# Group-norm coefficients of an input in fewer stages, averaged straight to the partition groups, with the third group's chain 24 steps later: a four-direction scan kernel on one core

## The chip, the cores and the metric

The kernel runs on one core of a Trainium2 chip. The metric is the device time of one execution in microseconds, median of the runs; lower is better. Engines are called PE (TensorE), DVE (VectorE), ACT (ScalarE), POOL (GpSimd) and SP (SyncE, which here only issues DMAs).

## The reference, cut to what matters

The input `x` is 32 x 48 x 64 x 128 (batch, channel, height, width), float32. Two layers do the same thing with different weights: the layer's input is group-normalised (16 groups of 3 channels), four recurrent scans run over it (down and up over the 64 rows with one set of weights, right and left over the 128 columns with two more), and the result is added to the layer's input.

```python
def _gn(v, G=16, eps=1e-5):
    g = v.reshape(B_, G, C_ // G, H_, W_)
    m = jnp.mean(g, axis=(2, 3, 4), keepdims=True)
    s = jnp.var(g, axis=(2, 3, 4), keepdims=True)
    return ((g - m) / jnp.sqrt(s + eps)).reshape(v.shape)

def step(w, b):
    def f(carry, inp):
        nxt = inp + _conv1d(carry, w, b)      # 5 taps over the other axis, 48 channels to 48
        return (nxt, nxt)
    return f
...
x = x + _L0_conv_ref(_gn(x), ...)             # down, up, right, left
x = x + _L1_conv_ref(_gn(x), ...)
```

A step needs the whole step before it, so the scans are serial: 63 + 63 row steps and 127 + 127 column steps for each layer and batch group.

## The kernel before, in words

**Tiling.** The batch of 32 is cut into four groups of 8 images (`GB = 8`, called the first to the fourth group below, `g` = 0 to 3 in the code). Row scans take one group at a time, column scans a pair of groups. The order of these phases is the list `PHASES` (L75): rows of group 0, rows of group 1, columns of the pair (0, 1), rows of group 2, and so on through both layers, 2286 steps in all. A vector of one step (8 of 48 channels by width or height folded in) lies as three tiles of 128 partitions by 128 elements (`NG = 3`); `step` (L654) makes the next vector with nine matrix products (two matmul records each in the profile) into three PSUM tiles, and three DVE additions (L674, PSUM plus bias plus the input vector) that write it back into the arena in SBUF. The next step's products read that.

**The order of the work.** Everything beside the scan is written into an agenda by hand: `at(t, fn, ...)` (L744) says that `fn` is issued just before scan step number `t`, counted through all phases (`starts` holds each phase's first number: 0, 126, 252, 506, ...). `spread(t, gen, every)` (L747) issues a generator's pieces, one at each `yield`, `every` steps apart. `catch_up` (L1082) issues what is due before each step, and `in_order` (L204) makes every engine execute its instructions in exactly the order in which they are issued. An engine's instruction that has to wait therefore holds up all that is queued behind it on that engine, the scan's own products and additions included.

**Statistics of an input.** Group norm of layer 0 needs mean and variance of each channel group of `x`. `InputStats` (L330) gathers them per channel and image:

- For the first group DVE does it (`take`, L343: `bn_stats` on pieces of 512 elements), before the scans start; eight `bn_aggr` (L378) at the end make mean and variance of each image, in the tile `mv_x`.
- For the other groups ACT does it (`take_others`, L349: a sum, L365, and a sum of squared deviations, L357, of each piece), spread over earlier phases; DVE turns the sums into mean and variance in three pieces of work (L383 to L385, L388 to L391, L393 to L398).

**From statistics to coefficients.** `scaling` (L263) then averages over the partitions of a channel group and spreads the result to the layout in which the scans hold a vector. `average` (L270) is a matrix product with `mask_sb`, whose entry is one over the number of partitions in the group where two partitions belong to the same group; `expand` (L274) is three products with `maskp`, which is the same mask with its columns rearranged (`spread_masks`, L253) for the three tiles of a vector. The chain for an input of layer 0 (`n == 1`, one mask), each stage ending at a `yield`:

1. PE: average of the means (L282).
2. DVE: copy to SBUF, `mean_c` (L285).
3. PE: expand (L287).
4. DVE: copy to SBUF, `mean` (L290); deviation from the average, squared, plus the variance (L295, L296, L297).
5. PE: average of that (L299).
6. DVE: copy, `var_c` (L302).
7. PE: expand (L304).
8. DVE: add epsilon (L307); ACT: square root (L310).
9. An empty stage, then DVE: reciprocal and a refinement (L314 to L319), scale and offset (L326, L327).

`ps` is one PSUM tile that holds all of these products. For results of layer 0, which feed layer 1, the same function runs with three masks (`n > 1`).

**Who uses the coefficients.** `scale_at_once` (L547, on DVE for the first four rows) and `scale_rows` (L535, on ACT, L543) apply them to rows in the arena before these are scanned. In `first_group` (L945), all of the start is written out: loads of `x` by image (`take_batch`), a permuted copy by POOL (`permute`, L491, its copies L500), a store to `xin` in DRAM (`put_out`) and a load of rows from there (`move_rows`); the first eight rows come by a matrix product instead (`rows_by_product`, L997).

**Around the third group.** `plan_input` (L757) plans loads, permuted copies and statistics of the other groups. For the third group (`g` = 2) the eight pieces are due from step 252 + 16 on, 13.5 steps apart; the last line of `plan_input` (L775) starts its `scaling` at the last piece's time plus `work + lag` = 12 plus 8. These steps lie in the first column phase, whose left scan begins at step 379. In the same stretch `plan_cols` (L812) plans what is done with the left scan's results: from step 379 + 34 on, POOL adds the residual to each unit of 128 x 2048 elements (`add_residual`, L599, L602), a quarter of the width at a time from the right, six units a quarter, and ACT and DVE take the result's statistics from them. The third group's rows are first scaled at step 506 - 13.

Of the kernel before, what the change touches and what calls it, by code (L numbers as in the profile page):

```python
# [35 lines left out]
P = ODD + C  # L36
# [5 lines left out]
GB = 8  # L42
E8 = 8
FULL = 128
NG = E8 * C // FULL
# [46 lines left out]
def kernel(  # L92
# [8 lines left out]
    nc = tc.nc  # L101
# [158 lines left out]
    def stat_tile(shape, name, key):  # L260
        return stat_pool.tile(shape, F32, tag=name, name=f"{name}_{key}")

    def scaling(key, layer, g, averages, masks):  # L263


        n = len(masks)
        yield from averages(key)
        mean_p, var_p = averages.result

        def average(ps, rhs):  # L270
            for i in range(n):
                nc.tensor.matmul(ps, masks[i], rhs[:, i], start=i == 0, stop=i == n - 1)

        def expand(ps, rhs):  # L274
            for o in range(NG):
                nc.tensor.matmul(ps[:, o], maskp[:, o], rhs, start=True, stop=True)

        def small(name):
            return stat_tile([FULL, NG, GB], name, key)

        ps = ps_stat.tile([FULL, 2 * NG + 2, GB], F32, tag="ps_stat", name=f"ps_{key}")
        average(ps[0:P, 0], mean_p)  # L282
        yield
        mean_c = stat_tile([P, GB], "mean_c", key)
        nc.vector.tensor_copy(mean_c, ps[0:P, 0])  # L285
        yield
        expand(ps[:, 1 : 1 + NG], mean_c)  # L287
        yield
        mean = small("mean")
        nc.vector.tensor_copy(mean, ps[:, 1 : 1 + NG])  # L290
        at = mean if n > 1 else mean_c.unsqueeze(1)
        np_ = FULL if n > 1 else P
        spare = small("dev")
        dev = spare[0:np_, 0:n]
        nc.vector.tensor_tensor(dev, mean_p, at, ALU.subtract)  # L295
        nc.vector.tensor_tensor(dev, dev, dev, ALU.mult)  # L296
        nc.vector.tensor_tensor(dev, dev, var_p, ALU.add)  # L297
        yield
        average(ps[0:P, 1 + NG], dev)  # L299
        yield  # L300
        var_c = stat_tile([P, GB], "var_c", key)
        nc.vector.tensor_copy(var_c, ps[0:P, 1 + NG])  # L302
        yield
        expand(ps[:, 2 + NG :], var_c)  # L304
        yield
        var = small("var")
        nc.vector.tensor_scalar(var, ps[:, 2 + NG :], GN_EPS, None, ALU.add)  # L307

        std = small("std")
        nc.scalar.activation(std, var, AF.Sqrt)  # L310
        yield
        yield
        r0 = std
        nc.vector.reciprocal(r0, std)  # L314
        t0 = spare
        nc.vector.tensor_tensor(t0, var, r0, ALU.mult)
        nc.vector.tensor_tensor(t0, t0, r0, ALU.mult)
        yield
        nc.vector.tensor_scalar(t0, t0, -0.5, 1.5, ALU.mult, ALU.add)  # L319
        scale, offset = (  # L320
            stat_pool.tile(
                [FULL, NG, GB], F32, tag=f"{t}{layer}{g}", name=f"{t}{layer}{g}"
            )
            for t in ("scale", "offset")
        )
        nc.vector.tensor_tensor(scale, r0, t0, ALU.mult)  # L326
        nc.vector.scalar_tensor_tensor(offset, mean, -1.0, scale, ALU.mult, ALU.mult)  # L327
        coeffs[layer, g] = scale, offset

    class InputStats:  # L330
# [2 lines left out]

        def __init__(self, key, nv):
            self.nv = nv
            if nv:
                self.st = stat_tile([P, nv, NBN * 6], "bn", key)
            if nv < GB:
                self.sum, self.neg, self.dev2 = (
                    stat_tile([P, GB, NBN], f"{n}_x", key)[:, nv:] for n in ("sum", "neg", "dev2")  # L340
                )

        def take(self, i, nat, b):  # L343

            for n in range(nat.shape[-1] // BN):
                at = slice(6 * (i + n), 6 * (i + n + 1))
                nc.vector.bn_stats(self.st[:, b, at], nat[:, b, n * BN : (n + 1) * BN])

        def take_others(self, i, nat):  # L349
            k = nat.shape[-1] // BN  # L350
            for square in (False, True):
                for b in range(self.nv, GB):
                    for n in range(k):
                        at = b - self.nv, slice(i + n, i + n + 1)
                        piece = nat[:, b, n * BN : (n + 1) * BN]
                        if square:
                            nc.scalar.activation(  # L357
                                junk[0:P],
                                piece,
                                AF.Square,  # L360
                                bias=self.neg[:, at[0], at[1]],
                                accum_out=self.dev2[:, at[0], at[1]],
                            )
                        else:
                            nc.scalar.activation(  # L365
                                junk[0:P],
                                piece,
                                AF.Identity,
                                accum_out=self.sum[:, at[0], at[1]],
                            )  # L370
                if not square:
                    at = slice(i, i + k)
                    nc.scalar.mul(self.neg[:, :, at], self.sum[:, :, at], -1.0 / BN)

        def __call__(self, key):
            mv = stat_tile([P, 1, GB, 2], "mv_x", key)
            for b in range(self.nv):
                nc.vector.bn_aggr(mv[:, 0, b], self.st[:, b])  # L378
            yield
            if self.nv < GB:  # L380
                n = GB - self.nv
                mean = stat_tile([P, GB], "mean_x", key)[:, 0:n]
                nc.vector.tensor_reduce(mean, self.sum, mybir.AxisListType.X, ALU.add)  # L383
                nc.vector.tensor_scalar(mean, mean, 1.0 / (NBN * BN), None, ALU.mult)
                nc.vector.tensor_copy(mv[:, 0, self.nv :, 0], mean)  # L385
                yield
                dev = self.neg
                nc.vector.tensor_tensor(  # L388
                    dev, dev, mean.unsqueeze(2).to_broadcast([P, n, NBN]), ALU.add
                )  # L390
                nc.vector.tensor_tensor(dev, dev, dev, ALU.mult)  # L391
                yield
                nc.vector.scalar_tensor_tensor(  # L393
                    dev, self.dev2, 1.0 / BN, dev, ALU.mult, ALU.add
                )
                var = stat_tile([P, GB], "var_x", key)[:, 0:n]
                nc.vector.tensor_reduce(var, dev, mybir.AxisListType.X, ALU.add)
                nc.vector.tensor_scalar(mv[:, 0, self.nv :, 1], var, 1.0 / NBN, None, ALU.mult)  # L398
                yield
            self.result = mv[:, :, :, 0], mv[:, :, :, 1]  # L400
# [68 lines left out]
    x_masks = [mask_sb]  # L469
# [274 lines left out]
    def at(t, fn, *args):  # L744
        agenda.append((t, len(agenda), fn, args))

    def spread(t, gen, every):  # L747


        def go(t):  # L750
            if next(gen, "end") != "end":
                at(t + every, go, t + every)
                agenda.sort(key=lambda a: a[:2])

        at(t, go, t)

    def plan_input(g, times, work, lag, nats, perms):  # L757

        stats = InputStats(f"x{g}", 0)
        rows = nats[0].shape[-1] // W  # L760
        ahead, pieces_of = len(nats), rows * W // BN
        per = rows * W * GB // perms[0].shape[-1]
        for j, t in enumerate(times):
            nat = nats[j % ahead]
            if j == 0 and g > 1:
                at(t - 7, take_in, g, 0, nat)
            for i in range(per):
                perm, r = perms[i % len(perms)], i * rows // per
                at(t + i * work / per, permute, nat, r, perm, [nc.gpsimd])
                at(t + i * work / per + 4, put_out, g, 2 * rows * j + r, perm, rows)  # L770
            at(t + lag, stats.take_others, pieces_of * j, nat)
            if j + ahead < len(times):
                free = t + 7
                at(free, take_in, g, 2 * rows * (j + ahead), nat)
        spread(t + work + lag + (0, 2, 8, 5)[g], scaling(f"x{g}", 0, g, stats, x_masks), 1)  # L775

    def plan_rows(k, t0, prev):
        if k == 1:
# [166 lines left out]
    def first_group():  # L945
# [26 lines left out]
        for b in range(2 * GB):  # L972
# [3 lines left out]
            i, b = divmod(b, GB)  # L976
# [6 lines left out]
        stats = InputStats("x0", GB)  # L983
# [56 lines left out]
        spread_masks()  # L1040
        for b in range(GB):
            stats.take(NBN // 2, parts[1], b)
        for r in range(12, 16):
            put_row(0, r)
        move_rows(0, 8, 16, False)
# [100 lines left out]
```

## Time and profile before

| what | value |
|---|---|
| three runs | 4352.66, 4369.14, 4376.32 us; median 4369.14 |
| profiled execution | 4367.57 us, of which the span from first to last instruction is 4365.80 |
| granted PE clock, mean | 0.982 |
| PE busy | 4150.5 us (95%) |
| DVE, ACT, POOL busy | 2169.3, 1337.3, 888.3 us |
| DMA queues | 680.34 MB, most of it in packets under 512 B |
| first scan step starts | 102.13 us after the span's start |
| first column phase | right scan from 658.95, left scan from 917.88 to 1191 us |

The page of the profile gives each engine's busy time, then groups of instructions by source line. A timeline line reads: start in us from the span's start, duration in us, engine, line, operation, written tile <- read tiles, shapes, count, and in brackets the idle time of the engine just before and what ended it. A line with a count above one is several like instructions in a row, and its duration is from the first one's start to the last one's end. A list of waits gives the engine and line that waited, what it waited for, and the total in us, the number of times and the longest.

### The profile page before, as it was taken

The page shows a single profiled execution, that of the slowest core. Times are in us where ns is not written, and L with a number is a line of the kernel's source. Part 1 is how long each engine was busy: PE and PEld are TensorE (multiplying, and loading weights), DVE is VectorE, ACT ScalarE, POOL GpSimd, SP SyncE. Part 2 cuts the span into 40 slices and gives each one's busy share as a digit, 9 for nine tenths or more (in the row PEclk, how much of TensorE's full clock was granted, in tenths as well). Part 3 has the DMA queues.
Part 4 walks back from the last instruction along what each step waited for, and adds up shares of the span by engine and source line. Part 5 has one row for each costly group of instructions (what it writes and reads, how often), then busy time and mean ns, then how long its engine had stood idle before and what let it go on. Part 6 is the DMA issues. An engine that isn't in the chain of part 4 may idle for free. (4 is left out here: it accounts for less than half of the span.)

```text
span 4365.8 us, 90057 instructions
## 1 busy us (share of the span) xinstructions
PE 4150.5 (95%) x36632; PEld 4121.9 (94%) x36632; DVE 2169.3 (50%) x6558; ACT 1337.3 (31%) x2656; POOL 888.3 (20%) x859
## 2 busy tenths in 40 slices
PE   4899989989999999999999999999999999999992
PEld 2899989989999999999999999999999999999992
DVE  6444444446665444444446665444444444444443
ACT  1583201435785545100006764503000012110122
POOL 4561010324322020010004410000000024510352
PEclk9999999999999999999999999999999999999996
DMA  9999699866999989579307989839188049999999
GB/s 187 176 195 165 104 159 168 216 121 206 228 195 152 159 158 156 92 126 199 80 1 244 224 163 143 124 61 170 32 139 181 1 88 237 238 242 157 170 199 178
DMA packets 2112607, 680.34 MB, mean 156 GB/s; under 512 B 2000448, under 2 KB 2052032, under 8 KB 2072256
## 3 DMA queue, kind: packets, MB, share of 16 engines
q1 hardware_dynamic: 2014176, 582.29, 70.9%
q10 hardware_dynamic: 94816, 86.00, 9.7%
q0 software_dynamic: 3200, 6.30, 0.6%
q8 instruction: 288, 4.72, 0.5%
q14 instruction: 127, 1.04, 0.1%
HBM read 397.57 MB, written 295.99 MB: 159 GB/s over the span
## 5 line engine op out<-in xcount | busy, mean ns | idle before, releaser
L543 ACT ACTIVATE arena<-arena,offset,scale 128x256 f32<-128x256 f32 (+2 forms) x816 | 576.8, 800 | 391.1 <-DVE arena L674 145.7
L602 POOL TENSOR_TENSOR arena<-arena 128x2048 f32<-128x2048 f32 x80 | 362.9, 4550 | 1509.8 <-PE step_10l L665 484.9
L500 POOL COPY arena<-arena 112x256 f32<-112x256 f32 x458 | 270.5, 648 | 549.6 <-DMA arena<-in_x 277.2
L665 PE MATMUL step_00r<-arena,early 128*128 128x128 f32 x2286 | 259.0, 277 | 15.3 <-DMA arena<-upa 15.2
L665 PEld LDWEIGHTS step_00r<-arena,early 128*128 128x128 f32 x2286 | 258.3, 194 | 16.0 <-issue 15.3
L434 ACT ACTIVATE early<-arena 128x256 f32<-128x256 f32 x192 | 129.4, 674 | 468.7 <-DMA arena<-xin 328.6
L665 PE MATMUL step_01r<-arena,early 128*128 128x128 f32 x2286 | 258.5, 277 | 14.5 <-DMA arena<-upa 14.5
L665 PEld LDWEIGHTS step_01r<-arena,early 128*128 128x128 f32 x2286 | 258.1, 193 | 14.9 <-issue 14.6
L665 PE MATMUL step_00l<-arena,wleft 128*128 128x128 f32 x2286 | 258.6, 276 | 13.9 <-DVE arena L674 13.9
L665 PEld LDWEIGHTS step_00l<-arena,wleft 128*128 128x128 f32 x2286 | 257.7, 193 | 14.1 <-DVE arena L674 14.1
L665 PE MATMUL step_11r<-arena,early 128*128 128x128 f32 x2286 | 259.3, 277 | 7.8 <-DVE arena L674 7.8
L665 PEld LDWEIGHTS step_11r<-arena,early 128*128 128x128 f32 x2286 | 258.6, 194 | 8.4 <-DVE arena L674 8.2
L665 PE MATMUL step_10r<-arena,early 128*128 128x128 f32 x2286 | 256.0, 275 | 0.0
L665 PEld LDWEIGHTS step_10r<-arena,early 128*128 128x128 f32 x2286 | 255.7, 192 | 0.3
L665 PE MATMUL step_10l<-arena,wleft 128*128 128x128 f32 x2286 | 255.5, 275 | 0.0
L665 PE MATMUL step_11l<-arena,wleft 128*128 128x128 f32 x2286 | 255.5, 275 | 0.0
L665 PE MATMUL step_01l<-arena,wleft 128*128 128x128 f32 x2286 | 255.4, 275 | 0.0
L665 PEld LDWEIGHTS step_10l<-arena,wleft 128*128 128x128 f32 x2286 | 255.4, 192 | 0.0
L665 PEld LDWEIGHTS step_11l<-arena,wleft 128*128 128x128 f32 x2286 | 255.4, 192 | 0.0
L665 PEld LDWEIGHTS step_01l<-arena,wleft 128*128 128x128 f32 x2286 | 255.3, 192 | 0.0
L627 ACT COPY arena<-arena 128x256 f32<-128x256 f32 x172 | 99.5, 654 | 420.1 <-POOL arena L602 143.1
L365 ACT ACTIVATE early<-arena 112x512 f32<-112x512 f32 x192 | 121.1, 631 | 296.1 <-DMA arena<-in_x 226.8
(179 smaller groups left out, 7113.1 us busy)
## 6 DMA issues: line engine op xcount, KB each, us to landing
arena<-in_x SPq DMA_DIRECT2D x48, 768.0 KB, 12.7
xin<-arena SPq DMA_DIRECT2D x96, 384.0 KB, 5.6
arena<-xin SPq DMA_DIRECT2D x96, 384.0 KB, 8.2
mid<-arena SPq DMA_DIRECT2D x96, 384.0 KB, 7.7
arena<-mid SPq DMA_DIRECT2D x192, 192.0 KB, 4.4
upb<-arena SPq DMA_DIRECT2D x192, 192.0 KB, 3.9
arena<-upb SPq DMA_DIRECT2D x96, 384.0 KB, 11.7
arena<-xin SPq DMA_DIRECT2D x186, 192.0 KB, 4.3
```

Of the source, the lines that this page charges most:

```text
L365: nc.scalar.activation(junk[0:P], piece, AF.Identity, accum_out=self.sum[:, at[0], at[1]],)
L434: nc.scalar.activation(junk[:, 0:n], view[:, b], AF.Identity, accum_out=self.sum[:, i, j : j + 1])
L500: copy(dst[:, r, q], src[:, r0 + r, q])
L543: nc.scalar.activation(args[0], args[0], AF.Identity, bias=args[2], scale=args[1])
L602: eng.tensor_tensor(unit, unit, nat, ALU.add)
L627: copy(by_w(perm)[:, a], src[:, a])
L665: nc.tensor.matmul(part(whole(ps[o]), -s), weights[:, i, FULL * (o - NG * s - i + 1) : FULL * (o - NG * s - i + 2)], part(src(i), s), star ...
```

## The change

Three edits, all for inputs of layer 0 (`n == 1`); the results' path with three masks keeps its instructions and their order.

- In `scaling`, `expand` is applied to the means themselves, right after the average and in the same stage, and later to the deviations themselves; the average of the deviations and its copy `var_c` are gone. `mean` is copied from PSUM after the second expansion has been issued. The chain has three stages fewer.
- For the first group, the aggregate of each image (`bn_aggr`) is issued right after that image's last `bn_stats` (`aggregate`), and no longer for all eight at the end. `mv_x` becomes a tile of the object for all groups.
- In `plan_input`, the third group's `scaling` starts 32 steps after the last piece's `work + lag`, where it was 8.

```diff
         average(ps[0:P, 0], mean_p)
+        if n == 1:
+            expand(ps[:, 1 : 1 + NG], mean_p[:, 0])
         yield
         mean_c = stat_tile([P, GB], "mean_c", key)
         nc.vector.tensor_copy(mean_c, ps[0:P, 0])
         yield
-        expand(ps[:, 1 : 1 + NG], mean_c)
-        yield
+        if n > 1:
+            expand(ps[:, 1 : 1 + NG], mean_c)
+            yield
         mean = small("mean")
-        nc.vector.tensor_copy(mean, ps[:, 1 : 1 + NG])
+        if n > 1:
+            nc.vector.tensor_copy(mean, ps[:, 1 : 1 + NG])
...
-        average(ps[0:P, 1 + NG], dev)
-        yield
-        var_c = stat_tile([P, GB], "var_c", key)
-        nc.vector.tensor_copy(var_c, ps[0:P, 1 + NG])
-        yield
-        expand(ps[:, 2 + NG :], var_c)
+        if n == 1:
+            expand(ps[:, 2 + NG :], dev[:, 0])
+            nc.vector.tensor_copy(mean, ps[:, 1 : 1 + NG])
+        else:
+            average(ps[0:P, 1 + NG], dev)
+            yield
+            var_c = stat_tile([P, GB], "var_c", key)
+            nc.vector.tensor_copy(var_c, ps[0:P, 1 + NG])
+            yield
+            expand(ps[:, 2 + NG :], var_c)
         yield
...
+            self.mv = stat_tile([P, 1, GB, 2], "mv_x", key)
...
+        def aggregate(self, b):
+            nc.vector.bn_aggr(self.mv[:, 0, b], self.st[:, b])
...
         def __call__(self, key):
-            mv = stat_tile([P, 1, GB, 2], "mv_x", key)
-            for b in range(self.nv):
-                nc.vector.bn_aggr(mv[:, 0, b], self.st[:, b])
+            mv = self.mv
...
-        spread(t + work + lag + (0, 2, 8, 5)[g], scaling(f"x{g}", 0, g, stats, x_masks), 1)
+        spread(t + work + lag + (0, 2, 32, 5)[g], scaling(f"x{g}", 0, g, stats, x_masks), 1)
...
             stats.take(NBN // 2, parts[1], b)
+            stats.aggregate(b)
```

## The prediction

> **What bounds the kernel now.** I read the page first. TensorE (PE) is the bound by far: 36,632 matmul records, 4150.5 us of a 4365.8 us span.
>
> ```profile
> PE 4150.5 (95%) x36632; PEld 4121.9 (94%) x36632; DVE 2169.3 (50%) x6558; ACT 1337.3 (31%) x2656; POOL 888.3 (20%) x859
> ```
>
> The line doesn't say what a change is worth, only that PE's pauses are what can be won: 215 us, 61 of them ahead of the first scan step at 102.13. So I listed next what PE itself waits for (us in total, times, longest).
>
> ```profile
> PE step_00l L665 <- DVE arena L674: 13.9, 1, 13.9
> PE step_00d L665 <- DVE arena L674: 13.1, 2, 8.5
> PE ps_x L272 <- DVE mv_x_x L378: 12.1, 1, 12.1
> ...
> PE ps_x L272 <- DVE dev_x L297: 4.7, 1, 4.7
> ```
>
> The first is in the left scan of the first column phase, the others at the start. Why did VectorE (DVE) give nothing to step_00l? Its timeline there:
>
> ```profile
> 928.13 0.35 DVE L674 SCALAR_TENSOR_TENSOR arena<-step_00l,bd,arena 128x128 f32<-128x128 f32 x1 [0.30 <-PE step_00l L665]
> 940.14 0.22 DVE L383 TENSOR_REDUCE mean_x_x<-sum_x_x 112x8 f32<-112x64 f32 x1 [11.66 <-ACT early L365]
> 940.40 3.07 DVE L384 TENSOR_SCALAR mean_x_x<-mean_x_x 112x8 f32<-112x8 f32 x1
> 943.50 0.17 DVE L385 COPY mv_x_x<-mean_x_x 112x8 f32<-112x8 f32 x1
> ...
> 947.16 0.23 DVE L388 TENSOR_TENSOR neg_x_x<-neg_x_x,mean_x_x 112x64 f32<-112x64 f32 x1 [2.72 <-ACT early L357]
> ```
>
> The third group's reduce (L383) stands in DVE's queue after left step 4 (from 0; each step is 18 matmul records and 2.01 us) and waits for ScalarE's (ACT's) last sums; the scan's own adds (L674) stand behind it. And L384, eight elements wide, takes 3.07 us instead of 0.17. GpSimd (POOL) says why:
>
> ```profile
> 934.15 9.29 POOL L500 COPY arena<-arena 112x256 f32<-112x256 f32 x16 [16.70 <-DMA arena<-in_x]
> 1000.18 27.11 POOL L602 TENSOR_TENSOR arena<-arena 128x2048 f32<-128x2048 f32 x6 [56.74 <-PE step_00l L665]
> ```
>
> POOL's copies end at 943.44, L384 at 943.47. The second line matters for what follows: six residual additions without a gap, 4.52 us each, released by PE.
>
> **What the Trainium skill says.** "SBUF — State Buffer", section "Who interferes with whom": a DVE instruction with two SBUF inputs contends with a GpSimd instruction that reads SBUF, and a copy or tensor_scalar in a 2-port mode contends too; the first holds the shared pair for its whole instruction. "VectorE: DVE Perf Modes", section "Mode 2×_2P — use both read ports for one tensor", adds that PSUM sources can't use that mode. The trace agrees: L384 above; L295 (two SBUF inputs) 4.15 us at the start against 0.15 for the same line at 957.58; the PSUM copy L290 0.18 in the same POOL run; the scan's add (one input PSUM) 0.35 beside POOL. The trace adds what the page doesn't say, in two forms. In both cases just told DVE waited through the rest of POOL's run, many copies. In the second group's chain each of these waited for one copy only (0.64 us):
>
> ```profile
> 318.78 0.51 DVE L384 TENSOR_SCALAR mean_x_x<-mean_x_x 112x8 f32<-112x8 f32 x1
> ...
> 319.33 0.55 DVE L385 COPY mv_x_x<-mean_x_x 112x8 f32<-112x8 f32 x1
> ...
> 320.57 0.53 DVE L388 TENSOR_TENSOR neg_x_x<-neg_x_x,mean_x_x 112x64 f32<-112x64 f32 x1
> 321.13 0.56 DVE L391 TENSOR_TENSOR neg_x_x<-neg_x_x 112x64 f32<-112x64 f32 x1
> ```
>
> The two that starved (DVE passed over again and again) asked 0.06 and 0.10 us before POOL's next start (89.92, 940.50), these about 0.4 us or more before it (319.21, for one).
>
> **The change part by part.** I go by the profiled execution: 4367.57 us, span 4365.80; the median of the runs is 1.6 higher.
>
> *Start, first group.* (Times us from the span's start.) Seven of eight aggregates (L378: 1.97/8 = 0.25 us each) go into gaps of 1.5 to 5.8 us that bn_stats spends waiting for in_x: PE gets the averages 1.65 us sooner; uncovered they'd cost 1.7. One average with its copy (0.54 + 0.2 + about 0.1 of handing over) leaves the variance half, an expansion (1.42) leaves the way to L295. If L295 still starves until POOL ends at 93.98, only about 0.6 is left of this; if it waits copy by copy, the scan starts up to 4.6 sooner. (L297 at 88.4 after three copies, expansion to 89.9, L316 to L327 five copies' waits to 93.6, L554 3.5: 97.5 instead of 102.1.) Either way row 16 is late next; here are ACT's, DVE's and POOL's timelines, a fence each:
>
> ```profile
> 128.46 0.62 ACT L543 ACTIVATE arena<-arena,offset,scale 128x128 f32<-128x128 f32 x1 [7.90 <-DMA arena<-xin]
> 135.28 23.56 ACT L543 ACTIVATE arena<-arena,offset,scale 128x128 f32<-128x128 f32 x46 [2.26 <-DMA arena<-xin]
> ```
>
> ```profile
> 145.56 0.35 DVE L674 SCALAR_TENSOR_TENSOR arena<-step_00d,bd,arena 128x128 f32<-128x128 f32 x1 [9.76 <-ACT arena L543]
> ```
>
> ```profile
> 100.64 3.69 POOL L500 COPY early<-arena 112x256 f32<-112x256 f32 x4 [6.66 <-DMA xin<-early]
> ```
>
> ACT waits for rows that come through POOL's permutes and SP's queue, none of which needs the coefficients; PE's 8.54 us pause there swallows the gain. What passes: the four copies in the last line took 3.69 instead of 2.34 beside DVE's L554, and all later permutes follow without a gap. If L554 is done sooner, up to 1.35 comes back. I take -0.7, between -1.4 and 0.
>
> *Second and fourth group.* One PE average less, 0.13 each (step starts 324.34 to 324.47). The chain ends three steps sooner. For the second, L316 to L327 move from about 345 to about 339, into POOL's copies (332.0 to 341.5): one copy's wait each, as at 318.78, where a step grew by 0.10 to 0.14; about 0.3; starved, 3. The fourth has no POOL work near (1622.7 on). Together +0.1, between -0.3 and +3.
>
> *Third group, 24 steps later: what goes.* Step 5 starts at 927.93, step 8 at 950.24: 22.31 for three steps of 2.01 and an average of 0.13, so 16.15 was lost. ACT's statistics end at 947.1 and depend on in_x, not on PE. By the order of instructions of the changed kernel the reduce now stands after left step 28, natural start of 29 at 927.93 + 24 x 2.01 = 976: all is ready. With one average less: -16.3. The moved work issues no DMA; on ACT it passes no other instruction, on POOL and SP it has none; scale_rows needs the coefficients at step 493, the chain ends by 419.
>
> *What comes in its place.* Count from T, the end of left step 31 (about 982). POOL's L602 for quarter 3 waits only for that step's read of column 96: before, it began at 1000.18 when step 32 began at 1000.11. The residuals have landed by about 971, where the DMA engines fall idle, so it again starts at T + 0.07 and its operations end at about 4.6, 9.1, 13.6, 18.2, 22.7, 27.2. PE runs average and expansion (0.13 + 0.59) ahead of step 32; L295 to L297 follow DVE's adds of step 33, 0.55 into step 34: T + 0.72 + 4.02 + 0.55 = T + 5.3, inside the second operation, 3.7 before the next. The trace has no such DVE operation beside an L602. The lower bound is 0 (POOL might let go within its 4.5 us; no gain possible, as nothing is removed); the upper is the whole run. By the second group's rows I take one operation for each: L295 at 9.1, L296 at 13.6, L297 at 18.2. PE's next expansion, queued ahead of step 35, waits for L297, and DVE's adds of step 34 are queued behind it: step 35 starts at 18.2 + 0.05 + 0.6 = 18.85 instead of 7.34, a loss of 11.5. L316, near 25.7, waits once more to 27.2: 1.2. In all +12.7. Beyond 27.2 POOL waits for quarter 2. ACT's square root delays the result statistics behind it by some 12 us; POOL's next run is 60 us off, enough cover.
>
> Sum: -0.7 + 0.1 - 16.3 + 12.7 = -4.2: 4363.4, or 4365.0 by the median.
>
> **The rivals.** *The lock is no lock here* (0.17): POOL lets go within an operation. For it: no row shows L602 holding DVE. Against: seven rows with copies, and the page. -4.2 - 12.7 = -16.9: 4352.2.
> *Only L295 waits, the two behind it slip in* (0.13): L297 at 9.5, step 35 at 10.15, 2.8 lost, later 1.0: -13.1, 4356.0. Against it: 319.33 and 321.13, seconds in a row that waited again.
> *L295 starves through POOL's run* (0.2), on the other side: L297 at 27.65, step 35 at 28.35, 21.0 lost, nothing later: -0.7 + 0.1 - 16.3 + 21.0 = +4.1, 4373.2, slower. For it: the two starved rows. Against: they asked within 0.1 us of POOL's next start. It decides from a new wait of 16.9 us.
>
> **Numbers.** Forecast (one operation each) 0.5: 4365. A measurement of this kernel can tell about 0.5%, 22 us, from no change, and its three runs spread over 24 us. Range 4348 to 4379: from the lockless case to the starved one, and some 5 us of spread. Faster by over 0.5% needs the lockless case and luck, 0.11; slower 0.04; within, 0.85.
>
> **What would show it.** Right: no pause near 930; L295, L296 and L297 of the third group last some 3.8, 4.5 and 4.5 us, PE pauses near 989 to 1001 for dev; row 16 still waits for ACT near 145. Wrong: L295 at 0.2 us there (4352), or about 22 us (4373); the pause of row 16 gone, so that the start pays up to 4.6.

## The result, and the profile after

| | before | after |
|---|---|---|
| median of 20 runs each | 4366.91 us (4351.00 to 4383.66) | 4364.42 us (4353.77 to 4371.49) |
| ratio after to before | | 0.9993, 95% interval 0.9982 to 1.0004 |
| span of the profiled execution | 4365.8 us | 4362.4 us |
| first scan step starts | 102.13 us | 96.57 us |
| left scan of the first column phase starts | 917.88 us | 921.38 us |
| rows of the third group start | 1191.06 us | 1192.01 us |

There is no difference that the measurement can tell: its interval reaches some 0.11% to either side, where the forecast had allowed for 0.5%. The forecast was 4365.0. The time says little, then, on whether the sum behind it held, so I went through its parts. The page of the kernel after (busy time of the engines, first line):

```profile
PE 4148.9 (95%) x36624; PEld 4119.6 (94%) x36624; DVE 2178.5 (50%) x6554; ACT 1337.5 (31%) x2656; POOL 887.7 (20%) x859
```

PE has as much work as before: 2024 scan steps of 18 matmul records (eight row phases of 126 steps, four column phases of 254; the 2286 given as the number of steps further up is the number of records of one column scan), and the statistics' products. But DVE, with four instructions fewer, is busy 9.2 us longer: instructions that wait inside count as busy. What PE itself waits for (total, times, longest), in the list of waits of the kernel after:

```profile
PE step_00d L675 <- DVE arena L684: 17.1, 2, 11.2
...
PE step_01d L675 <- DVE arena L684: 13.1, 1, 13.1
PE ps_x L276 <- DVE dev_x L301: 12.7, 2, 11.0
```

Before's wait of 13.9 us in step_00l is no longer in the list. In its place PE waits 11.0 us for `dev_x` (L301 is before's L297, L299 and L300 its L295 and L296, L684 its L674). DVE's timeline of the kernel after shows both ends of the exchange:

```profile
980.14 0.21 DVE L393 TENSOR_REDUCE mean_x_x<-sum_x_x 112x8 f32<-112x64 f32 x1
980.39 0.17 DVE L394 TENSOR_SCALAR mean_x_x<-mean_x_x 112x8 f32<-112x8 f32 x1
...
991.07 3.71 DVE L299 TENSOR_TENSOR dev_x<-mv_x_x,mean_c_x 112x8 f32<-112x8 f32 x1
994.81 4.42 DVE L300 TENSOR_TENSOR dev_x<-dev_x 112x8 f32<-112x8 f32 x1
999.27 4.42 DVE L301 TENSOR_TENSOR dev_x<-dev_x,mv_x_x 112x8 f32<-112x8 f32 x1
1003.61 0.85 DVE L684 SCALAR_TENSOR_TENSOR arena<-step_00l,bd,arena 128x128 f32<-128x128 f32 x3
```

The reduce (L393, before's L383) has no idle time ahead of it now, where it had 11.66 us, and L394 takes 0.17 us where L384 took 3.07. But ten microseconds later three instructions, eight elements wide, take 12.5 us together. The scan's own additions (L684) come behind them. POOL's timeline of the kernel after:

```profile
936.77 9.47 POOL L510 COPY arena<-arena 112x256 f32<-112x256 f32 x16 [16.69 <-DMA arena<-in_x]
985.77 26.87 POOL L612 TENSOR_TENSOR arena<-arena 128x2048 f32<-128x2048 f32 x6 [39.53 <-PE step_00l L675]
```

The residual additions run from 985.77 without a gap, 26.87 / 6 = 4.48 us each, so that their ends lie near 990.2, 994.7, 999.2 and 1003.7. DVE's three instructions end at 994.78, 999.23 and 1003.69: each waited for the end of one POOL instruction.

What followed on PE is seen in its timeline, and in the table of windows, whose columns after the length are the busy times of the five engines, and PE's granted clock third from the end:

```profile
1003.74 1.45 PE L276 MATMUL ps_x<-dev_x,maskp 112*128 112x8 f32 x6 [10.96 <-DVE dev_x L301]
```

```profile
1005.70:1007.70 2.00, 2.00 (x11) 2.00 (x11) 0.17 (x1) 0.00 (x0) 2.00 (x1) 0.50 1.12 340
1007.70:1009.00 1.30, 1.30 (x8) 1.30 (x7) 0.53 (x2) 0.00 (x0) 1.30 (x2) 0.50 1.01 189
1009.00:1011.00 2.00, 2.00 (x20) 2.00 (x19) 1.05 (x4) 1.08 (x4) 2.00 (x1) 0.98 0.93 225
```

PE pauses for 10.96 us, and then works at half its clock from 1003.74 to about 1009, which loses another 2.65 us: 13.6 together. By the starts of the steps the loss is 13.8 (11.8 up to step 35, 2.0 in it).

At the start, the lines that answer those shown of before are, for DVE (the additions that wait for row 16) and POOL, a fence each:

```profile
142.00 0.35 DVE L684 SCALAR_TENSOR_TENSOR arena<-step_00d,bd,arena 128x128 f32<-128x128 f32 x1 [12.46 <-ACT arena L553]
```

```profile
99.56 2.40 POOL L510 COPY early<-arena 112x256 f32<-112x256 f32 x4 [6.77 <-DMA xin<-early]
```

SP issues the loads of row 16 and those after it; before and after:

```profile
121.65 19.88 SPq L200 DMA_DIRECT2D arena<-xin  x20
```

```profile
119.26 19.96 SPq L200 DMA_DIRECT2D arena<-xin  x20
```

The first step is 5.56 us sooner, but DVE waits longer for row 16 (12.46 us, where it was 9.76): of the 5.56, 3.56 are left there. POOL's four copies take 2.40 us instead of 3.69.

### The profile page after: what moved, and what is told of

Its sections match the earlier page's. It is cut to its first block, busy times and chain, and to the rows that moved or that the text cites. A ratio compares the mean times of both kernels' runs of the same rounds, so it can differ in the third digit from the quotient of the medians.

```text
span 4362.4 us, 90034 instructions
## 1 busy us (share of the span) xinstructions
PE 4148.9 (95%) x36624; PEld 4119.6 (94%) x36624; DVE 2178.5 (50%) x6554; ACT 1337.5 (31%) x2656; POOL 887.7 (20%) x859
## 6 DMA issues: line engine op xcount, KB each, us to landing
arena<-in_x SPq DMA_DIRECT2D x48, 768.0 KB, 12.8
```

## The experiments

My theory was the forecast's: the old loss in the third group is gone, and in its place three DVE instructions wait for one POOL addition each, because their inputs both lie in SBUF; that POOL run is all that keeps the change from gaining. The main rival: some other thing at the later place, or the shortened chain itself, holds the time up. In all ratios below, each kernel is compared with the kernel before on the same chip; before's medians there were 4358.88 us (first four), 4357.61 (next four) and 4359.90 (last three). The ratios and their intervals are those on record; they are not the quotients of the medians, from which they differ by up to 0.0006. Where nothing is said, a kernel computes all of the reference.

**The third group's chain elsewhere.** Three places beside the 32 of the change: ahead of POOL's run, four steps into a worse place, and between POOL's first run and its second.

```diff
-        spread(t + work + lag + (0, 2, 32, 5)[g], scaling(f"x{g}", 0, g, stats, x_masks), 1)
+        spread(t + work + lag + (0, 2, 20, 5)[g], scaling(f"x{g}", 0, g, stats, x_masks), 1)
```

(28 and 54 in the two others.)

> The changed kernel with the third group's chain 12 steps later than in the kernel before instead of 24 (offset 20). All of its DVE instructions then lie after ACT's last sums and before POOL's first residual addition. Port theory: no pause of PE between left steps 4 and 45, each of the chain's DVE operations at 0.15 to 0.3 us; the 13.9 us lost there by the changed kernel (11.8 ahead of step 35, 2.0 behind it) come back: 4364.4 - 13.9 = 4350.5 us. Rival (the pause comes with the shortened chain, since PE's second expansion now stands directly behind DVE's work, wherever the chain is put): the pause is there again, 4364 us.

Measured: 4346.20 us, ratio 0.9973 (0.9960 to 0.9986). All of the chain's operations took 0.15 to 0.29 us (947.38 to 969.6), POOL's additions began after them at 978.68, and PE had no pause in the left scan.

> The changed kernel with offset 28, four steps earlier than it has. The deviations (L299 to L301) then come ahead of POOL's first residual addition, the reciprocal's group (L324 to L335: five operations with two SBUF inputs or one in a 2-port mode) inside POOL's run. Port theory: L299 to L301 at 0.2 us; L324 and L325 wait for an addition each, and the three behind step 34's adds wait again: losses of about 8.1 + 2.0 + 7.6 + 2.0 = 19.7 us in place of 13.9, so worse than the changed kernel although nearer to where the statistics are ready: 4364.4 + 5.8 = 4370.2 us. Rival (shortened chain): 4364 us. Rival (any time after the sums are ready is free): 4350.5 us.

Measured: 4367.96 us, ratio 1.0020 (1.0011 to 1.0029), slower than before. The deviations were done ahead of POOL's run (from 979.84 on, 0.15 to 0.17 us each), and the second half of the chain was caught in it. POOL's and DVE's timelines of this kernel:

```profile
984.13 26.91 POOL L612 TENSOR_TENSOR arena<-arena 128x2048 f32<-128x2048 f32 x6 [43.03 <-PE step_00l L675]
```

```profile
988.88 4.28 DVE L324 TENSOR_TENSOR dev_x<-var_x,std_x 128x24 f32<-128x24 f32 x1
993.19 4.44 DVE L325 TENSOR_TENSOR dev_x<-dev_x,std_x 128x24 f32<-128x24 f32 x1
998.34 3.80 DVE L327 TENSOR_SCALAR dev_x<-dev_x 128x24 f32<-128x24 f32 x1
1002.17 4.44 DVE L334 TENSOR_TENSOR scale<-std_x,dev_x 128x24 f32<-128x24 f32 x1
1006.65 4.44 DVE L335 SCALAR_TENSOR_TENSOR offset<-mean_x,scale 128x24 f32<-128x24 f32 x1
```

Five instructions wait for five additions. Four steps earlier is 8 us worse, since five operations of the chain fall into the run where three did: the left scan took 278.7 us, 21.8 over its undisturbed 256.9, where the changed kernel's lost 13.8.

> The changed kernel with offset 54: the chain lies between POOL's first run of residual additions (six, ending about 27 us after left step 31) and its second (from left step 63 on). Port theory: no pause, 4350.5 us, the same as for offset 20, though it is the latest of all; ACT's square root stands behind the result statistics of three units and may come some us late without anybody waiting. Rival (the later the chain, the more it collides): 4364 us or more.

Measured: 4342.51 us, ratio 0.9967 (0.9955 to 0.9979). The chain ran from 1018.75 on in 0.15 to 0.29 us an operation, between the runs of POOL.

**The lock itself.** The place of the change (32), but each of the small operations of an input of layer 0 gets one operand or its result in PSUM, so that no more than one input lies in SBUF. The deviations are computed twice, once into PSUM (`way`) and once into SBUF (`dev`), so that their square has one input in each.

```diff
+        way = dev
+        if n == 1:
+            way, at = ps[0:P, 1 + NG : 2 + NG], ps[0:P, 0:1]
+            nc.vector.tensor_tensor(way, mean_p, at, ALU.subtract)
         nc.vector.tensor_tensor(dev, mean_p, at, ALU.subtract)
-        nc.vector.tensor_tensor(dev, dev, dev, ALU.mult)
-        nc.vector.tensor_tensor(dev, dev, var_p, ALU.add)
+        nc.vector.tensor_tensor(way, dev, way, ALU.mult)
+        nc.vector.tensor_tensor(dev, way, var_p, ALU.add)
...
-        var = small("var")
+        var = in_psum[0] if n == 1 else small("var")
...
-        t0 = spare
+        t0 = in_psum[1] if n == 1 else spare
...
+        mean = ps[:, 1 : 1 + NG] if n == 1 else mean
```

> The changed kernel at its own offset, 32, with the chain's intermediate results kept in PSUM, so that no DVE operation from the deviations to the offset has two SBUF inputs or a 2-port mode (one more small operation[...]). Place, order and number of steps stay. Port theory: the deviations at about 0.2 us each inside POOL's run, no pause ahead of step 35, 4350.5 us. Rival (DVE is slowed by POOL whatever it reads, or PE waits for another reason): unchanged, 4364 us.

Measured: 4345.46 us, ratio 0.9975 (0.9966 to 0.9984). POOL's and DVE's timelines of this kernel:

```profile
981.85 27.10 POOL L618 TENSOR_TENSOR arena<-arena 128x2048 f32<-128x2048 f32 x6 [46.89 <-PE step_00l L681]
```

```profile
987.35 0.16 DVE L304 TENSOR_TENSOR dev_x<-mv_x_x,ps_x 112x8 f32<-112x8 f32 x1
987.54 0.17 DVE L305 TENSOR_TENSOR ps_x<-dev_x,ps_x 112x8 f32<-112x8 f32 x1
987.75 0.17 DVE L306 TENSOR_TENSOR dev_x<-ps_x,mv_x_x 112x8 f32<-112x8 f32 x1
```

The same operations, at the same steps, in the middle of the same POOL run, take 0.16 to 0.17 us and not 3.7 to 4.4; PE doesn't pause, and the left scan takes 256.9 us. Only the place of the operands was changed and one small operation added, so the wait in the changed kernel is DVE's and POOL's over SBUF; the later place and the shortened chain by themselves cost nothing there.

**The parts of the change by themselves.** The stages and early aggregates alone (32 put back to 8), and the later place alone (in the kernel before, 8 made 20).

> The fewer stages and the early aggregates alone; the third group's chain starts where it did before (8). Theory (what is gained in the third group is the later place alone, and the earlier first step is given back by row 16 and the second group's pauses): the 16 us between left steps 4 and 8 are lost again, first scan step near 96.6, time 0 to 1 us below before, ratio 0.999 to 1.000. Rival (the first step's 5.6 us reach the end): 5.5 us below before, ratio 0.9987 with its interval under 1.

Measured: 4356.76 us, ratio 0.9994 (0.9981 to 1.0007). The ratio fits the theory, but its reason does not: the left scan lost 8.6 us (265.5 for 256.9), not 16. The rival's 0.9987 lies in the interval too, though not its "interval under 1", so what the earlier start is worth isn't settled by this run.

> The old chain with all its stages, in the kernel before, with the third group's start 12 steps later (20 where it was 8). Theory (the delay past ACT's last sums gives back the whole 16.2 us, and a chain that ends before POOL's residual additions pays nothing in their place): ratio 0.9963, some 16 us below before, no pause of PE over 2 us between left steps 4 and 40. Rival (the fewer stages are needed for it, or a later wait takes the place): ratio 0.998 or above.

Measured: 4348.45 us, ratio 0.9977 (0.9966 to 0.9988), by the ratio some 10 us less. This is a miss: the left scan took its undisturbed 257.0 us, no other pause had come, and yet 6 of the 16.2 us were missing. The rival's bound (0.998) isn't met either.

**Both kernels again.** No edits; the changed kernel timed a second time, and a second profile of the kernel before.

> The changed kernel itself a second time, beside the others on this chip. Theory: ratio 0.999 (0.998 to 1.000); in its profile the third group's three deviations take 3.7, 4.4 and 4.4 us again, each through one of POOL's residual additions. Rival (the one operation each was an accident of one execution): one of the three starves through several additions (over 9 us) or slips in under 1 us.

Measured: 4358.66 us, ratio 0.9998 (0.9987 to 1.0009); the deviations took 3.73, 4.42 and 4.42 us. The one operation each came again and is no accident.

> The kernel before, a second profile. Theory: the deviation of the first group starves again (about 4 us at the start), the first scan step is near 102, 16 us are lost in left steps 4 to 8, and the pause near 420 us lies between 6 and 13 us, so that its 8.5 in the first profile was one draw of several. Rival: that pause is 8.5 again within 0.5, so the changed kernel's 13.1 is the change's own.

Measured: 4364.34 us; the first step at 102.66; 15.9 us lost in the left scan; the pause near 420 us lasted 12.8 us, where before's first profile had 8.5. So the 13.1 us of the changed kernel at that place are not the change's own.

**What the old loss was.** After these runs I compared POOL's last run of permuted copies (L500, sixteen copies) in all profiles. Its start, counted from the first step of the left scan, went from 1.3 to 16.3 us. From that came a new theory, tried on two more profiles of the kernel before.

> The kernel before, a third profile. Theory (what the third group's chain cost before is set by how late POOL's last permuted copies of its piece come after the left scan's first step; in ten profiles so far they began 1.3 to 16.3 us after it, 10.1 on average, and where the chain still stood at 8, starts of 16.3, 15.9 and 8.7 went with losses of 16.3, 16.0 and 8.7): the time lost in the left scan, over the 256.9 us that it takes undisturbed, equals that start within 1 us, whatever it is. Rival (the loss is a fixed 16 us): 16 again even where the copies begin earlier or later.

> The kernel before, a fourth profile. Theory and rival as for the third: a loss within 1 us of the time from the left scan's first step to the start of POOL's last run of permuted copies, against a fixed 16 us.

Measured: 4356.38 and 4357.16 us. For the third profile, POOL's and PE's timelines:

```profile
928.91 9.34 POOL L500 COPY arena<-arena 112x256 f32<-112x256 f32 x16 [14.97 <-DMA arena<-in_x]
```

```profile
919.90 12.22 PE L665 MATMUL step_00l<-arena,wleft 128*128 128x128 f32 x108
...
1186.02 14.23 PE L665 MATMUL step_02d<-arena,early 128*128 128x128 f32 x126
```

The copies begin 928.91 - 919.90 = 9.0 us after the left scan, which takes 1186.02 - 919.90 = 266.1, that is 9.2 over 256.9. All profiles with the chain at its old place:

| profile | copies begin after the left scan's start | lost in the left scan |
|---|---|---|
| before, first | 16.3 us | 16.3 us |
| before, second | 15.9 | 15.9 |
| before, third | 9.0 | 9.2 |
| before, fourth | 12.8 | 12.9 |
| stages only | 8.7 | 8.6 |

The rival, a fixed 16 us, is out. The old loss follows the lateness of the third group's last piece, which changes from one execution to the next. ACT's last sums, which the reduce waits for, begin when that piece has landed; ACT's timeline of before's first profile:

```profile
934.11 0.63 ACT L365 ACTIVATE early<-arena 112x512 f32<-112x512 f32 x1 [13.21 <-DMA arena<-in_x]
```

POOL's copies begin at 934.15, with them. For a lateness under 8.7 us, which four of the thirteen profiles had (1.3 to 8.0), there is no profile with the chain at its old place: that the loss equals it there too is not shown.

**Both cures together.** The PSUM operands, and the third group's chain at 54.

> The changed kernel with one operand of each small operation in PSUM and the third group's chain at 54 where it was 32: neither a lock nor a late sum can hold it, and the second group's 4.2 us operation is gone too. Theory (each cure alone takes out the whole 13.85 us, so together they give no more, and the second group's 3 us are swallowed by the pause near 420): ratio 0.997, between 0.996 and 0.998. Rival (the second group's operation reaches the end, 3 us more): 0.9963 or below, under the later chain's 0.9967.

Measured: 4345.10 us, ratio 0.9963 (0.9951 to 0.9975). It beats both kernels, as the earlier and the later place and the PSUM operands alone do. By its median it lies on the rival's bound, and its interval holds both cases; the trace speaks for the theory, since its second group's up scan begins at 518.74 us, no sooner than in the kernels where one operation of that group took 4.2 us (512.12 to 517.74). I call it undecided; the four good versions can't be told apart. Nor can any of them be told from the later place alone in the kernel before (0.9977, 0.9966 to 0.9988), whose interval overlaps with each of theirs: that the fewer stages add anything to it is not shown.

## Why the prediction was right, and where it wasn't

The terms can be set against all nine timed comparisons. Three of them, from the profiles: the start, with all up to the left scan, is worth -2.4 (it begins at 919.6 on average in five profiles with the old start, 917.1 in eight with the new one); the old loss is 10.4 on average (135.8 / 13, the copies' lateness in all thirteen profiles); at 32 the new one is 13.8, at 28 it is 21.8.

| kernel | sum of the terms | as a ratio | measured |
|---|---|---|---|
| the change | -2.4 - 10.4 + 13.8 = +1.0 | 1.0002 | 0.9993; again 0.9998 |
| at 28 | -2.4 - 10.4 + 21.8 = +9.0 | 1.0021 | 1.0020 |
| at 20; at 54 | -2.4 - 10.4 = -12.8 | 0.9971 | 0.9973; 0.9967 |
| PSUM; PSUM at 54 | -12.8 | 0.9971 | 0.9975; 0.9963 |
| stages only | -2.4 | 0.9994 | 0.9994 |
| delay only | -10.4 | 0.9976 | 0.9977 |

Each lies in the measured interval. The old loss is put at the lateness for all of them, also where the table above doesn't reach. (With the mean lateness of the five profiles of the old start alone, 12.1, every sum with the old loss in it falls by 1.7 us, and all still do.)

*Start, forecast -0.7 (-1.4 to 0), "row 16 is late next".* The mechanism was right: DVE still waits for row 16 there, and most of the gain stays in that wait. "If it waits copy by copy" was what came: L299 to L301 took 0.34, 0.54 and 0.54 us. Measured from POOL's scaling of the mask (L257), which takes the loads' own arrival out, the first step came 18.4 us after it in four of the five profiles with the old start and 14.03 in six with the new one (PSUM operands aside): 4.4 sooner, where I had bounded it at 4.6. But in the fifth with the old start, the fourth profile of before, where L295 waited for one copy only, it came 15.12 after it. So some 3.3 of the 4.4 are L295's long wait, which the old start can also be without, and 1.1 are left for the fewer stages and the early aggregates. Row 16's loads, the SP line above, came 37.8 and 36.8 us after it on average: 1.0 sooner. That is what passes, within the forecast's range, and POOL's four copies (2.40 us for 3.69) are where the forecast had it come from. The whole -2.4 lies outside that range; the rest of it is in the loads: L257 itself began at 84.2 on average with the old start and at 82.5 with the new one (80.2 to 86.3). Whether the change does that or the draw of executions, thirteen profiles don't settle.

*Second and fourth group, forecast +0.1, starved +3.* Both cases occurred. In the changed kernel L324 to L335 took 0.41 to 0.56 us each; in the kernels at 20, 28 and 54, DVE's L327 starved, as here in the first of them:

```profile
334.69 4.20 DVE L327 TENSOR_SCALAR dev_x<-dev_x 128x24 f32<-128x24 f32 x1
```

The third group's chain comes 600 us later, so I take this for the case of an execution; but it came in all three of these profiles and in none of the three with the same second-group chain at 32 and at 8, and a second profile of each, which could tell, wasn't taken. PE paused 3.0 us there, and then only 6.0 to 6.5 us near 420 instead of 12 to 13.5, so nothing of it is seen to reach the end; why that pause is shorter by more than 3 us is open. The forecast had the size, but not the pause that swallows it.

*Third group, "16.15 was lost", -16.3.* This is the term that was mis-sized. The mechanism was right (reduce behind ACT's sums, the scan's additions behind the reduce), and in every kernel that moved it the loss went. But I took the size from one execution as if it stood in each. With the chain at its old place it was 8.6 to 16.3 us in five profiles; the lateness that it followed there is 10.4 on average of thirteen, between 1.3 and 16.3. The hint was in the profile: ACT's wait named a transfer, and here what waited for that transfer changed from one execution to the next.

*In its place, +12.7.* 13.8 was measured, twice. Counted from T, the end of step 31 (985.70; POOL's run began at T + 0.07, as forecast), the forecast had L295 to L297 end at 9.1, 13.6 and 18.2; they ended at 9.1, 13.5 and 18.0. Two smaller terms were wrong, in opposite directions. The later wait of L316 (1.2) didn't come, as POOL's run ended at 1012.64 and L324 followed at 1013.88. And PE's half clock after the pause, 2.65 us, part of which hid in the 0.6 I had for the expansion (1.3 measured), wasn't in the sum, though the old loss showed it: 0.50 between 943.9 and 946 in the kernel before, and 0.89 between 947 and 951. The Trainium skill has it in "TensorE: Matmul & The Clock Gate", section "Part 1: The HAM clock gate (the "warmup" mystery)": the array's clock is halved after an idle window of about 3.4 us, and comes back after about as long a busy one. The trace agrees on the half clock; here it lasted 5.3 us. In the kernel at 20 the clock stayed at 1.00 after the pause of 3.0 us in the second group, and was 0.50 after one of 6.3 us near 415.

*The sum.* -4.2 was forecast; the terms as measured make about +1, and the ratios say -1 to -3, with some 5 us to either side. The old loss, 6 too large, was made up for in part by a start 1.7 larger than forecast. That the time came within 1 us of 4365.0 is luck: the sum as measured lies 5 us above the forecast one, and the median of before that the forecast started from, of three runs, was 2.2 us above that of the twenty.

*The rivals.* "The lock is no lock here" and "only L295 waits" are out by L299 to L301, twice. "L295 starves through POOL's run" is out for this place, though DVE starved elsewhere.

## What to carry to other kernels

Before moving a small DVE operation, look at what POOL runs at the new place: with two SBUF inputs each such instruction can cost a whole POOL instruction, in a chain one after the other, and the scan behind it stands still; giving it one operand in PSUM took that away without moving it. A loss read from one profile, whose wait names a transfer, can be a draw, as it was here: read it in several profiles before it goes into a sum. And a long pause of PE costs more than its length, since the clock is halved when it starts again: here 2.65 us on top of 10.96.

## What the runs showed of the hardware that I had not expected

The Trainium skill, "SBUF — State Buffer", section "Who interferes with whom", says that the one who comes first holds the shared pair for its instruction. With the additions of 4.5 us that is what was seen, eleven times in three profiles: each of DVE's instructions waited for one addition, and then had its turn. With POOL's short copies two things were seen, in the same instruction of the same code: the first group's L295 took 4.15 to 4.22 us, through the rest of POOL's run, in four profiles (three of the kernel before, one of the later place alone); in the fourth profile of the kernel before it waited for one copy:

```profile
92.30 0.30 DVE L295 TENSOR_TENSOR dev_x<-mv_x_x,mean_c_x 112x8 f32<-112x8 f32 x1
92.63 0.54 DVE L296 TENSOR_TENSOR dev_x<-dev_x 112x8 f32<-112x8 f32 x1
```

I count an instruction as asking from its start in the trace. By that, L295 and the reduce's successor (L384; L394 in the changed chain) asked 0.06 to 0.14 us before POOL's next copy in each of nine starved cases, and those that waited for one copy mostly 0.21 us or more before it. But L327 in the kernels at 20, 28 and 54 asked 0.36 us before the next copy and was passed over by three copies and two memsets, while it waited for one only when it had asked 0.33, 0.34 and 0.37 us before. So the moment of asking counts, but isn't all; what else decides stays open. What sets the lateness of the third group's last piece in an execution stays open too.
